# 528 small products and three 32x32 turns appended behind the last image

## The chip, the cores and the metric

The kernel runs on one core of one Trainium2 chip. The metric is the device time of one execution in microseconds (us). A profile of one execution is read beside it: its span runs from the first to the last instruction that the profiler recorded on the core.

## The reference

Thirty-two images of 384 channels and 28 x 28 points, in float32, pass through two layers. Cut to what matters:

```python
# layer 0, per image
y = depthwise_conv_7x7(x) + dw_b
y = layernorm_over_channels(y) * ln_g + ln_b
y = gelu(einsum('bhwc,cf->bhwf', y, w1) + b1)      # 384 -> 1536
nx = gx / (mean(gx) + eps), gx = sqrt(sum over points of y*y)
y = grn_g * (y * nx) + grn_b + y
x = x + einsum('bhwf,fc->bhwc', y, w2) + b2        # 1536 -> 384
# layer 1, per image
logits = [mean(x) @ W1.T, max(x) grouped, min(x) @ W3.T] @ Wfc.T
out = sigmoid(logits[:, :, None, None] + x)
```

## The kernel before

The kernel has two stages. In the first (`with ExitStack() as one`), which the trace shows up to about 500 us, the depthwise convolution of all images is done on TensorE with banded matrices, channel by channel, and the sums of weight blocks that the second stage multiplies by are formed and stored in DRAM. In the second stage each image goes through `up(b)` (384 to 1536 channels) and `down(b)` (1536 to 384). Both use fast matrix multiplication schemes: sums of blocks of the data are formed by VectorE and GpSimd, and TensorE multiplies each by a sum of weight blocks. `up` has 15 products per weight block group on 392 columns (line 979), `down` has 38 steps of 3 products on 196 columns (line 1139). All are float32. The names that matter here:

- `u2_tiles`: five buffers for the weights of `down`; the first has 128 partitions of 768 numbers and is named `u` in the profile (the fifth lies in `ws`).
- `d_room`: 128 x 8820 numbers that hold the block sums of `down`. GpSimd writes them in `sums` (line 1102).
- `room`: a work area that the sums of the last image use as well.
- `bank(name)`: the next of eight PSUM banks of 512 float32 columns, handed out in turn.
- `down` ends each image's products by adding them from PSUM into the image `xt` on VectorE, and reduces it to sums, maxima and minima (`stq`, `st`).
- `gate_store(b)` multiplies these by the gate weights on GpSimd (`zt`, line 1187), sums them over the partitions with one small product by ones (`pa`, line 1189), forms the logits on VectorE (`lt`, `lg`, lines 1193 and 1198), and applies the sigmoid on ScalarE, three times 128 x 784 (line 1200). For the last image each third is stored by SyncE as soon as it is ready (line 1204).

The order on each engine is mostly found by the framework's planner; an instruction wrapped in `tc.keep_in_program_order` keeps its place in the order in which the program was written. The last two lines of the loop over images, and the line behind it, are:

```python
        down(b, beside(b))
    gate_store(B - 1)
```

A float32 product of the program is one `nc.tensor.matmul`; the profile shows it as two records MATMUL, each with a LDWEIGHTS of its own in front.

Of the kernel before, what the change touches and what calls it, by code (L numbers as in the profile page):

```python
# [13 lines left out]
P = 128  # L14
# [4 lines left out]
HW = 28  # L19
# [12 lines left out]
PW = P // RW  # L32
# [183 lines left out]
def convnext_gate_kernel(  # L216
# [13 lines left out]
    nc = tc.nc  # L230
# [57 lines left out]
    room = const.tile([P, CB * NT + NA * NH], F32, name="room")  # L288
# [101 lines left out]
    with ExitStack() as one:  # L390
# [107 lines left out]
        keep = tc.keep_in_program_order  # L498
# [282 lines left out]
        for s in range(NK):  # L781
# [8 lines left out]
            if s in later:  # L790

                dst, src = later[s]
# [15 lines left out]
            if s == NK - 1:  # L808
# [19 lines left out]
                for half, (b0, b1) in enumerate(((0, B0), (B0, B))):  # L828
# [4 lines left out]
                    for n in range(2 * PAIRS):  # L833
                        i, c2 = divmod(n, PAIRS)
# [10 lines left out]
            elif s < NK - 2:  # L845
                for c2 in range(PAIRS):
# [9 lines left out]
                    elif q in (2 * PAIRS + 2, 2 * PAIRS + 5, 2 * PAIRS + 8):  # L856
                        n = FB + 4 * ((q - 2 * PAIRS) // 3)
# [35 lines left out]
    u2_tiles = [up2.tile([P, UD * KD * P], F32, name=f"u2_{i}") for i in range(NU2 - 1)]  # L893
# [6 lines left out]
    d_room = dp.tile([P, SLOTS * KD * NQ4], F32, name="d_room")  # L900
# [11 lines left out]
    def bank(name):  # L912
        nonlocal nbanks
        nbanks += 1
        return pszs[(nbanks - 1) // 4 % 2].tile([P, 512], F32, tag="pz", name=name)
# [265 lines left out]
    def gate_store(b):  # L1181

        xt, st = gates.pop(b)
        ov = out[b].rearrange("(cb p) n -> p cb n", p=P)
        n = NQ * R
        zt = smp.tile([P, NQ, R], F32, tag="zt", name=f"zt_{b}", bufs=1)
        nc.gpsimd.tensor_tensor(zt, gate, st.unsqueeze(2).to_broadcast([P, NQ, R]), ALU.mult)
        pa = bank(f"pa_{b}")
        nc.tensor.matmul(
            pa[:, :n], ones_f, zt.rearrange("p q r -> p (q r)"), start=True, stop=True  # L1190
        )
        lt = smp.tile([P, CB, n], F32, tag="lt", name=f"lt_{b}", bufs=1)
        nc.vector.tensor_tensor(
            lt, fct.rearrange("p cb q r -> p cb (q r)"),
            pa[:, :n].unsqueeze(1).to_broadcast([P, CB, n]), ALU.mult,
        )
        lg = smp.tile([P, CB], F32, tag="lg", name=f"lg_{b}")
        nc.vector.tensor_reduce(lg, lt, AX.X, ALU.add)
        for cb in range(CB):
            nc.scalar.activation(  # L1200
                xt[:, cb, :], xt[:, cb, :], AF.Sigmoid, bias=lg[:, cb : cb + 1], scale=1.0
            )
            if b == B - 1:
                nc.sync.dma_start(ov[:, cb, :], xt[:, cb, :])
        if b < B - 1:
            nc.scalar.dma_start(ov, xt)
# [3 lines left out]

    HF = FB // 2
    V, A = nc.vector, nc.scalar

# [11 lines left out]
    def squared(b):  # L1227

        return 0 if b == 1 else HF if b in (0, B - 1) else HF // 2

    def within(b):
        hooks, at = adder()
        p = b - 1
        if b == 0:
            at((0, 3), finish, 1)
            at((0, 13), finish, 2)
            at((0, 17), finish, 3)
            for i, m in enumerate(first_outs[:HF]):
                at((0, 29), stretch, m, nc.gpsimd)
# [8 lines left out]
        elif b == 1:  # L1248
            for i, m in enumerate(first_outs[HF:]):
                at((0, 2 * i), stretch, m, nc.gpsimd)  # L1250
# [10 lines left out]
        else:  # L1261
            for i, f in enumerate(order[HF:]):
                at((0, 5 + 2 * i), scale, p, f)
            for i in range(0, 13, 6):
                at((0, 4 + i), sums, p)
        if b > 1:
            for m in range(HF):
                at((2, 2 + 4 * m), gelu, b, m)
            for m in range(squared(b)):
                at((2, 29 if m >= HF // 2 else 22 + 2 * m), square, b, m)  # L1270
        if 2 <= b and b + 1 < B:
# [3 lines left out]
    def beside(b):  # L1275
        hooks, at = adder()
        n = b + 1
        last = n == B - 1

        def part(i):  # L1280

            return i * ND // 15

        if b + 2 < B:
            for cb in range(CB):
                at(2 + 3 * cb, normed, b + 2, (cb,))
            if b == 0:
                for i, d in enumerate(FORMS):
                    at(12 + 2 * i, forms_up, 2, (d[0],), V)
            else:  # L1290
                at("after sums", forms_up, b + 2)
        if n < B:
            g0 = 0 if n == 1 else HF
            for f in range(g0, FB):
                at(part((f - g0) // 3), gelu, n, f)
            s0 = squared(n)
            for f in range(s0, FB):
                at(part((1 if last else 3) + (f - s0) // 2), square, n, f)
        if n < B:
            at(part(4 if last else 9), grn, n)  # L1300
        if b >= 1 and not last:
            at(part(11) if n < B else ND - 8, gate_store, b - 1)
        if n < B:
            at(part(11) if b else 0, load_x, n)
        if last:
            for i, f in enumerate(order):
                at(part(4 + i // 3), scale, n, f, V if i % 3 == 2 else A)
            for i in range(part(7), ND):
                at(i, sums, n)
            if b >= 1:  # L1310
                at(part(9), gate_store, b - 1)
        elif n < B:
            for i, f in enumerate(order[:HF]):
                at(part(9) + 1 + i, scale, n, f)
        return hooks
# [14 lines left out]
    for b in range(B):  # L1330
        if b >= 1 and b + 1 < B:
            up(b + 1, within(b + 1))
        down(b, beside(b))
    gate_store(B - 1)


# [37 lines left out]
```

## Time and profile before

| | |
|---|---|
| median of the runs shown | 3040.19 us (two runs: 3039.02 and 3041.36) |
| the profiled execution, its own time | 3041.33 us |
| its span | 3039.6 us |
| granted TensorE clock, mean | 0.997 |
| TensorE products busy | 2996.2 us (99%), 14436 records |
| TensorE weight loads busy | 2427.9 us (80%), 14436 records |
| VectorE / ScalarE / GpSimd busy | 2036.2 / 1787.4 / 2431.9 us |
| last records: the product `pa` (line 1189) | starts at 3032.02 us |
| last sigmoid (line 1200) | ends at 3035.95 us |
| last data moved by the DMA engines | between 3038 and 3039 us |

Times inside the profile count from the start of the span. The granted clock is the share of full speed that TensorE's throttle passes, 1.00 being full. A record's duration covers the time from its start to the modelled end of its results; the next record can start earlier, so the distance from start to start, and not the duration, is what a stream of products costs.

### The profile page before, as it was taken

Reading aid. Unit: us, or ns where it says so; the run is one execution under the profiler, and the core shown is the slowest. Engines: PE = TensorE matmul, PEld = TensorE weight load, DVE = VectorE, ACT = ScalarE, POOL = GpSimd, SP = SyncE. Lnnn points to the kernel's source line nnn. Section 1 sums busy time; section 2 is a strip of 40 time slices with the busy share of each in tenths; the row PEclk is TensorE's granted clock in tenths of the full one; section 3 lists DMA queues with packets and bytes.
Section 4 is the critical chain, followed back from the end, with each engine's and each line's share of the span. In section 5 each row is a group of like instructions: output and inputs, shape, how many; then the busy total and the mean of one; then the engine's idle time right before and its main releaser. Section 6 shows DMA issues by size and latency. Waiting matters only on the chain.

```text
span 3039.6 us, 43826 instructions
## 1 busy us (share of the span) xinstructions
PE 2996.2 (99%) x14436; PEld 2427.9 (80%) x14436; DVE 2036.2 (67%) x4643; ACT 1787.4 (59%) x2899; POOL 2431.9 (80%) x1811
## 2 busy tenths in 40 slices
PE   8999999899999999999999999999999999999998
PEld 8999997577777777777777777777777777777777
DVE  5767667776666666666666666666666666666665
ACT  4455554756666666666666666665666666666661
POOL 3367866688888888888888888888888888888897
PEclk9999999999999999999999999999999999999999
DMA  9899997546666666666666565566655666666645
GB/s 358 327 359 375 364 342 259 169 149 203 199 206 207 201 204 207 199 206 207 199 206 207 198 205 194 199 203 204 195 191 196 197 198 200 201 203 201 195 152 198
DMA packets 279256, 674.94 MB, mean 222 GB/s; under 512 B 24234, under 2 KB 99704, under 8 KB 273016
## 3 DMA queue, kind: packets, MB, share of 16 engines
q1 hardware_dynamic: 266472, 634.63, 61.9%
q10 hardware_dynamic: 12560, 37.51, 3.1%
q8 instruction: 117, 1.92, 0.2%
q14 instruction: 107, 0.88, 0.1%
HBM read 575.57 MB, written 96.48 MB: 221 GB/s over the span
## 4 chain that ended last, share of the span: by engine, by line
PE 91%; POOL 3%; DVE 3%; DMA 2%; issue 1%; ACT 1%; SPq 0%; ACTq 0%; DVEq 0%; POOLq 0%
PE ph_C L979 13%; PE ph_A L979 12%; PE ph_B L979 12%; PE pz_A L1139 8%; PE pz_C L1139 8%; PE pz_D L1139 7%; PE pz_F L1139 7%; PE pc L718 5%; PE pc L720 4%; PE pc L722 4%; PE pt L516 2%; PE pz_H L1139 2%; PE pz_I L1139 2%; POOL d_room L1102 2%; PE pz_E L1139 2%; DVE room L344 1%
## 5 line engine op out<-in xcount | busy, mean ns | idle before, releaser
L355 ACT ACTIVATE y<-y,vecs,gsc 128x784 f32<-128x784 f32 x375 | 359.9, 1030 | 467.0 <-DVE gsc L1047 467.0
L1102 POOL TENSOR_TENSOR d_room<-y 128x588 f32<-128x588 f32 x250 | 360.1, 1444 | 294.4 <-PE pz_B L1139 217.7
L927 ACT ACTIVATE y<-y,b1f 128x784 f32<-128x784 f32 x384 | 350.4, 945 | 196.7 <-DVE y L998 174.7
L979 PE MATMUL ph_C<-room,ws 128*128 128x392 f32 x1224 | 456.6, 494 | 4.1 <-DVE y L996 2.9
L1102 POOL TENSOR_TENSOR d_room<-d_room,y 128x588 f32<-128x588 f32 x308 | 442.8, 1442 | 16.7
L979 PE MATMUL ph_B<-room,ws 128*128 128x392 f32 x1220 | 451.7, 492 | 2.3 <-DMA ws<-u1d 2.3
L979 PE MATMUL ph_A<-room,ws 128*128 128x392 f32 x1220 | 453.0, 492 | 0.1
L979 PEld LDWEIGHTS ph_C<-room,ws 128*128 128x128 f32 x1224 | 230.6, 190 | 182.2 <-DVE y L996 21.7
L979 PEld LDWEIGHTS ph_A<-room,ws 128*128 128x128 f32 x1220 | 231.6, 190 | 170.5 <-POOL room L386 0.8
L979 PEld LDWEIGHTS ph_B<-room,ws 128*128 128x128 f32 x1220 | 231.0, 190 | 164.0 <-DMA ws<-u1d 2.9
L741 POOL TENSOR_TENSOR stats<-stats,sq 128x896 f32<-128x896 f32 x96 | 200.8, 2092 | 176.6 <-ACT sq L735 175.9
L947 ACT ACTIVATE stats<-y 128x784 f32<-128x784 f32 x381 | 326.7, 858 | 9.1
L1102 POOL TENSOR_TENSOR d_room<-y,d_room 128x588 f32<-128x588 f32 x214 | 306.5, 1438 | 27.0 <-PE pz_D L1139 15.9
L386 POOL TENSOR_TENSOR room<-room 128x392 f32<-128x392 f32 x298 | 298.9, 1019 | 11.6
L735 ACT ACTIVATE sq<-yt,dwb 128x224 f32<-128x224 f32 x368 | 157.2, 474 | 223.3 <-DVE yt L725 212.9
L1102 POOL TENSOR_TENSOR y<-y 128x588 f32<-128x588 f32 x180 | 258.3, 1435 | 6.5
L994 DVE TENSOR_TENSOR y<-y,ph_B 128x392 f32<-128x392 f32 x252 | 135.6, 558 | 157.9 <-ACT y L927 123.5
L992 DVE TENSOR_TENSOR y<-y,ph_C 128x392 f32<-128x392 f32 x386 | 213.4, 561 | 25.0 <-PE ph_C L979 0.3
L725 DVE STREAM_TRANSPOSE yt<-pc 128x448 f32<-128x448 f32 x184 | 119.3, 648 | 138.0 <-PE pc L722 99.5
L1139 PE MATMUL pz_A<-d_room,u 128*128 128x196 f32 x1050 | 204.4, 330 | 0.4 <-DMA u<-u2d 0.2
L718 PE MATMUL pc<-xt,tmat 128*128 128x224 f32 x736 | 200.8, 355 | 0.6 <-ACT xt L527 0.6
L1139 PEld LDWEIGHTS pz_A<-d_room,u 128*128 128x128 f32 x1050 | 178.4, 190 | 8.6 <-POOL d_room L1102 0.9
(299 smaller groups left out, 6410.8 us busy)
## 6 DMA issues: line engine op xcount, KB each, us to landing
u<-u2d SPq DMA_DIRECT2D x487, 384.0 KB, 3.7
ws<-u1d SPq DMA_DIRECT2D x380, 320.0 KB, 3.0
tmat<-fs SPq DMA_DIRECT2D x47, 1420.0 KB, 10.5
ws<-u2d SPq DMA_DIRECT2D x121, 384.0 KB, 3.8
yi<-yd SPq DMA_DIRECT2D x95, 448.0 KB, 6.4
yd<-yt SPq DMA_DIRECT2D x47, 896.0 KB, 7.0
x<-in_x SPq DMA_DIRECT2D x32, 1176.0 KB, 5.4
out<-x ACTq DMA_DIRECT2D x31, 1176.0 KB, 6.3
```

The source lines that it names most:

```text
L355: eng.activation(out, in_, AF.Identity, bias=add, scale=mul)
L386: tc.keep_in_program_order(eng.tensor_tensor(d, o[in0], o[in1], op))
L718: keep(nc.tensor.matmul(po, t[:, c, P : 2 * P], xc, start=True, stop=False))
L735: nc.scalar.activation(sq[:, cy % SQ + ci], yt[:, cy + ci], AF.Square, bias=dwb[:, cc + ci : cc + ci + 1], scale=1.0,)
L741: ins = nc.gpsimd.tensor_tensor(ssum, ssum, sq, ALU.add)
L927: ins = nc.scalar.activation(y, y, AF.Gelu, bias=b1f[:, f : f + 1], scale=1.0)
L947: ins = nc.scalar.activation(stats[:, :NT], ys[b][:, f, :], AF.Square, accum_out=ssqs[b][:, f : f + 1])
L979: ins = nc.tensor.matmul(banks[t, bk][:, :NH], wts[t, g][:, gi, :], o[opnd], start=(first == 1), stop=True, skip_group_check=True,)
L992: ins = nc.vector.tensor_tensor(d, d, p, ALU.add)
L994: ins = nc.vector.tensor_tensor(d, d, p, ALU.subtract)
L1102: eng.tensor_tensor(d[0], o[a][0], o[c][0], ALU.add if sign == "+" else ALU.subtract)
L1139: nc.tensor.matmul(pz[:, :NQ4], wt[:, i % UD, t, :], o[opnd][0][:, t, :], start=(first and t == 0), stop=(t == KD - 1), skip_group_check=True,
```

## The change

One function is added and called once behind the last `gate_store`. It takes four PSUM banks (`tiled_0` to `tiled_3`) and issues 528 products in nine groups. Each multiplies a piece of `d_room` by a piece of the first weight buffer; both hold whatever the last image left there. A product's rows (the partitions that are summed over) start at partition `r`, and its columns are written to PSUM partitions from `j`. In the program each product carries the part of TensorE's 128 x 128 array that it uses: `tile_size` [rows, columns] and `tile_position` [r, j]. Nothing reads the four banks. Then VectorE turns 32 x 32 blocks of three overlapping pieces of `d_room` into `room`, which nothing reads afterwards either. The output is computed as before.

```diff
+    def tiled_products():
+
+        keep = tc.keep_in_program_order
+        probes = [bank(f"tiled_{i}") for i in range(4)]
+        nw = 0
+
+        def product(r, nr, j, ncol, out_bank, n, back=False):
+            nonlocal nw
+            w0 = 32 * (nw % 20)
+            m0 = 32 * (nw % 64)
+            nw += 1
+            rows_, cols_ = slice(r, r + nr), slice(j, j + ncol)
+            rhs = d_room[rows_, m0 : m0 + n]
+            if back:
+                rhs = rhs.rearrange("p (a b) -> p a b", b=28)[:, ::-1, ::-1]
+            keep(
+                nc.tensor.matmul(
+                    probes[out_bank][cols_, :n], u2_tiles[0][rows_, w0 : w0 + ncol], rhs,
+                    start=True, stop=True, skip_group_check=True,
+                )
+            )
+
+        for i in range(8):
+            for j in range(4):
+                product(0, P, 32 * j, 32, i % 4, 280)
+        for i in range(4):
+            for j in range(4):
+                for r in range(4):
+                    product(32 * r, 32, 32 * j, 32, r, 448)
+        for i in range(4):
+            for r in range(4):
+                for j in range(4):
+                    product(32 * r, 32, 32 * j, 32, r, 448)
+        for i in range(6):
+            for j in range(4):
+                for r in range(4):
+                    product(32 * r, 32, 32 * j, 32, r, 196)
+        for i in range(4):
+            for j in range(4):
+                for r in range(4):
+                    product(32 * r, 32, 32 * j, 32, r, 196, True)
+        for i in range(6):
+            for j in range(4):
+                for r in range(4):
+                    product(32 * r, 32, 32 * j, 32, r, 112)
+        for i in range(10):
+            for r in range(4):
+                product(32 * r, 32, 0, P, r, 224)
+        for i in range(6):
+            for j in range(4):
+                for r in range(2):
+                    product(64 * r, 64, 32 * j, 32, 2 * r + i % 2, 224)
+        for i in range(6):
+            for j in range(2):
+                for r in range(2):
+                    product(64 * r, 64, 64 * j, 64, 2 * r + i % 2, 224)
+        src = d_room[:, : HW * HW + 4]
+        for i in range(3):
+            src = d_room[:, i * 800 : i * 800 + HW * HW + 4]
+            view = bass.AP(
+                tensor=src.tensor, offset=src.offset, ap=[src.ap[0], [HW, HW], [1, PW]]
+            )
+            keep(
+                nc.vector.transpose(
+                    room[:, i * HW * PW : (i + 1) * HW * PW].rearrange("p (a b) -> p a b", b=PW), view
+                )
+            )
...
     gate_store(B - 1)
+    tiled_products()
```

## The prediction

> **What bounds the kernel now.** I read the page's busy shares first, then the chain of work that ended last, then its final twelve microseconds, because the whole change stands behind the last image.
>
> ```profile
> PE 2996.2 (99%) x14436; PEld 2427.9 (80%) x14436; DVE 2036.2 (67%) x4643; ACT 1787.4 (59%) x2899; POOL 2431.9 (80%) x1811
> PE 91%; POOL 3%; DVE 3%; DMA 2%; issue 1%; ACT 1%; SPq 0%; ACTq 0%; DVEq 0%; POOLq 0%
> ```
>
> TensorE is busy 99% of the span and carries 91% of the chain. So whatever TensorE gets behind its last record is added to the end, unless it fits beside what still follows there. What follows, in the chain of the last stretch (start, duration, what):
>
> ```profile
> 3031.30 0.23 DVE st L1176 x3
> ...
> 3032.02 0.46 PE pa L1189 x2
> 3032.48 0.02 issue
> 3032.50 0.39 DVE lt L1193
> 3032.89 0.02 issue
> 3032.91 0.39 DVE lg L1198
> 3033.30 0.02 issue
> 3033.33 0.95 ACT x L1200
> 3034.28 0.84 ACTq L1370
> 3035.11 0.84 ACT x L1200
> ```
>
> The reader is to see that TensorE's last product is `pa`, at 3032.02, and that logits, three sigmoids and three stores fill the remaining 7.6 us to the span's end at 3039.6. This is the only cover that the change has.
>
> For the price of a product I took the chain in a full stretch of `down` and of `up`:
>
> ```profile
> 3023.81 0.99 PE pz_H L1139 x6
> 3024.80 0.99 PE pz_D L1139 x6
> ```
>
> ```profile
> 2922.26 1.32 PE ph_A L979 x4
> 2923.58 1.32 PE ph_B L979 x4
> ```
>
> Six records of 196 columns start within 0.995 us (starts 3021.60 and 3020.60 tell the third digit), 165.8 ns each; four of 392 columns within 1.317 us, 329.2 ns each. The line through both is 0.834 ns a column plus 2.4 ns. Records of 192 and 224 columns in the first stage (162 and 189 ns) lie on it. A program's float32 product is two such records, one behind the other, each with its own weight load, which hides under the record before (loads of 128 columns last 190 ns, yet the starts stay 166 ns apart).
>
> **The change part by part.** It removes nothing and adds no DMA, and moves no instruction: in the changed kernel's order of instructions all 528 products stand on TensorE behind `pa`, and the three turns on VectorE behind `lg`. The first product waits for an earlier product of TensorE itself, long done, and nobody waits for the products or the turns.
>
> *The turns.* The trace has the turn of 128 x 448 numbers at 648 ns (line 725); one of 896 is then about 1.3 us, three 3.9 us. They start behind `lg`, at 3033.3, and end at 3037.2, beside the stores and the products: nothing on the path. Without that cover they would cost 3.9 us.
>
> *The instructions.* TensorE's 28872 records go with an instruction queue of 1.92 MB in 117 packets, about 67 bytes a record; 2112 more (two products and two loads each) are 9 packets. Spread over the products' time they come at least as seldom as one in some 13 us. I take zero; if each stopped TensorE for the 2.5 us that the nearest transfer takes to land (a store of 392 KB), 22 us.
>
> *The products, one after another.* Two records each by the line above:
>
> | group | products x columns | us |
> |---|---|---|
> | 128 x 32 parts | 32 x 280 | 15.1 |
> | 32 x 32, rows change first | 64 x 448 | 48.1 |
> | 32 x 32, columns change first | 64 x 448 | 48.1 |
> | 32 x 32 | 96 x 196 | 31.8 |
> | 32 x 32, read backwards | 64 x 196 | 21.2 |
> | 32 x 32 | 96 x 112 | 18.4 |
> | 32 x 128 | 40 x 224 | 15.1 |
> | 64 x 32 | 48 x 224 | 18.2 |
> | 64 x 64 | 24 x 224 | 9.1 |
> | sum | 528 | 225.1 |
>
> *How many run at once* is what this trace does not show: all its streams use the whole array (the nearest, three records of 24 rows, are single and use all 128 columns). From below: sixteen 32 x 32 parts fit the array, eight of 64 x 32, and four of each other size, so 167.6/16 + 18.2/8 + 39.3/4 = 22.6 us. From above: no overlap, 225.1 us; above that, if a load is not hidden and each record's results are waited for: 163 ns (329 less 166) and about 109 ns (the loads of 128 and 96 columns, 190 and 164 ns, continued to 32) on each of 1056 records, 287 us more.
>
> I take **two at once**, 112.6 us. The reason is the two records of a product. In the rows above records start in written order, and the second record of a product needs the part of the array that the first is still streaming through. So if starts stay in order, the second record waits for the first, and only the next product, in another part, can start beside it. Then each product costs one record instead of two. Every two neighbours of the nine groups use different parts, so this holds in all of them. To it I add one emptying of the pipe, 163 ns, at each of the five changes of the part's size: 0.8 us. Between two-fold and serial lies a weight load seen once per product, 109 ns x 528 = 58 us.
>
> [...]
>
> *The clock.* The trace shows its price:
>
> ```profile
> 2988.00:2990.00 2.00, 0.04 (x1) 0.07 (x1) 1.97 (x5) 0.00 (x0) 2.00 (x2) 0.93 0.97 386
> 2990.00:2992.00 2.00, 2.00 (x6) 2.00 (x7) 0.54 (x2) 0.00 (x0) 2.00 (x3) 0.50 0.20 80
> ```
>
> Here the seventh number of a stretch is the granted clock. After 5.0 us without a product (from 2984.96) it fell to 0.50, and six records of 196 columns took 2.09 us instead of 0.995, until it rose after some 3 us. In the last stretch it fell at about 3034.1; before, TensorE had only `pa` since 3029.8. The products fill the time from 3032.2, so I count full speed; a fall at the start would cost at most some 1.6 us.
>
> *Sum.* The first product starts at 3032.2 (`pa` holds TensorE for 0.17 us in the chain at 3022.59). 3032.2 + 112.6 + 0.8 + 0.2 for the last results is 3145.8, against 3039.6: plus 106.2 us. On the profiled execution's 3041.33 us that is 3147.5; this execution was 1.1 us above the median of 3040.19, so the median would be 3146.4. I say **3147 us**, 3.5% slower.
>
> **The rivals.**
>
> *No overlap.* Small parts are worth nothing here, or a stretch of float32 holds the whole array. For it: every record in this trace starts when the one before has streamed. Against it: the neighbours share no rows or no columns of the array. 3032.2 + 225.1 + 1.0 = 3258.3: plus 218.7, **3259 us**.
>
> *Four or more at once*, the rival on the other side. If each part has its own queue, the second record of a product does not hold the next one back. Four at once take 56.3 us: 3032.2 + 56.3 + 1.0 = 3089.5, plus 49.9, **3090 us**, 1.6%, not slower by 2%. It decides from 3.3 at once, where the products take 68 us. With all parts at once (22.6 us) it is 3056 to 3057 us. Against it are the two records of each product; nothing in the trace speaks for more than two.
>
> *Dearer than serial.* The throttle does not take a product in one sixteenth of the array for work: two-fold at half clock is 2.1 x 112.6 = 236 us, **3270 us**, serial at half clock 473 us, 3506 us; or the loads and results come into sight, up to 512 us, 3545 us. Against it: the clock stayed at 1.00 through stretches with a few narrow products (96 columns of weights, at 480 us), but no part was as small.
>
> *The change does nothing*, because what nobody reads is dropped: the order of instructions has all 528, so I give it no share.
>
> **How the numbers follow.** Two at once, with or without a load in sight (3147 to 3205): 0.50. No overlap: 0.20. Four at once: 0.15. More than four: 0.05. Dearer than serial: 0.10. The range takes in the first three, 3085 to 3265, which leaves 0.15 out. Two per cent, about what a measurement of this kernel can tell from no change, is 61 us: slower by more has the first, second and fifth case, 0.80; within it the others, 0.19; 0.01 is left for faster, since nothing is taken away.
>
> **What the changed profile would show.** Right: TensorE's `tiled` records start at 3032.2; two of them start per record time, so 96 products of 196 columns take about 16 us and 64 of 448 about 24; both groups of 448 take the same; the clock stays at 1.00; sigmoids, stores and turns keep their places and end by 3040. Wrong: the group where columns change first takes twice the one where rows change first (then only rows overlap), groups at the serial figure or at a quarter of it, or a granted clock of 0.50 behind 3034.

## The result

The changed kernel takes 3073.41 us, median of two runs (3072.26 and 3074.56), against 3040.19 us before: ratio 1.0109, 95% interval 1.0066 to 1.0153. A second comparison, told of below, gave 1.0098 (1.0081 to 1.0114). The kernel is slower by 30 to 33 us, half of the 2% that a reader would call a clear change and a third of the 106 us that were forecast. The time lies outside the forecast range, on its low side.

The busy line of the page and the line of TensorE's instruction queue (packets, MB, share) after the change:

```profile
PE 3029.8 (99%) x15492; PEld 2451.7 (80%) x15492; DVE 2039.9 (66%) x4646; ACT 1787.4 (58%) x2899; POOL 2433.4 (79%) x1811
...
q8 instruction: 125, 2.05, 0.3%
```

The records are 1056 more on TensorE, two for each of 528 products, and three on VectorE. The queue brought 8 packets more than the 117 before.

The chain that ended last, from `pa` on (start, duration, what):

```profile
3033.85 0.70 PE pa L1189 x2
3034.55 15.03 PE tiled L1229 x387
3049.58 0.49 issue
3050.07 2.34 PE tiled L1229 x108
3052.41 1.13 issue
3053.55 2.20 PE tiled L1229 x99
3055.75 1.55 issue
3057.30 1.78 PE tiled L1229 x95
3059.08 1.97 issue
3061.05 10.89 PE tiled L1229 x234
```

Logits, sigmoids and stores have left the chain; from `pa` to the end it is only products, and four stretches, 5.1 us in all, in which TensorE was idle and waited for nothing that the profile shows. `pa` itself starts at 3033.85 instead of 3032.02: 1.8 us of the difference of these two executions arose before the first added instruction. From the start of `pa` to the end of the span it is 39.0 us instead of 7.6. (The chain counts only the records that lie on it: x108 there is 128 records in the trace.)

The nine groups, one line for each in the order of the diff (start and end, length, TensorE busy, weight loads busy, granted clock, share of the DMA engines, GB/s):

```profile
3034.48:3039.76 5.28, 5.28 (x65) 2.28 (x65) 0.73 0.49 191
3039.76:3043.26 3.50, 3.50 (x133) 2.31 (x132) 1.00 0.16 61
3043.26:3047.04 3.78, 3.78 (x152) 2.83 (x130) 1.00 0.02 4
3047.04:3051.26 4.22, 3.73 (x214) 2.94 (x195) 1.00 0.03 8
3051.26:3054.73 3.47, 2.34 (x143) 1.68 (x139) 1.00 0.02 5
3054.73:3061.50 6.77, 3.26 (x207) 2.37 (x197) 0.98 0.01 2
3061.50:3067.00 5.50, 5.50 (x84) 5.07 (x80) 0.72 0.01 3
3067.00:3069.43 2.43, 2.43 (x100) 1.86 (x96) 1.00 0.03 7
3069.43:3071.93 2.50, 2.50 (x56) 1.73 (x48) 1.00 0.00 0
```

All products took 37.45 us. The two groups of 448 columns, 48.1 us each one after another, took 3.50 and 3.78: by an estimate from these figures some 13 products at once (48.1/3.50 = 13.7, 48.1/3.78 = 12.7). The three short groups (lines 4 to 6) took 14.46 us for 71.4 us of serial work, and TensorE was not even busy in all of it. The first and the seventh ran at a mean clock of 0.73 and 0.72.

The turns and the stores stand where they were expected, some 2 us later, as `pa` was (timeline, same execution: start, duration, engine, what):

```profile
3035.30 3.09 DVE L1276 STREAM_TRANSPOSE room<-d_room 128x896 f32<-128x896 f32 x3
...
3036.39 2.01 SPq L1204 DMA_DIRECT2D out<-x  x3
```

### The profile page after: what moved, and what is told of

Its sections match the earlier page's. It is cut to its first block, busy times and chain, and to the rows that moved or that the text cites. A ratio compares the mean times of both kernels' runs of the same rounds, so it can differ in the third digit from the quotient of the medians.

```text
span 3072.8 us, 45942 instructions
## 1 busy us (share of the span) xinstructions
PE 3029.8 (99%) x15492; PEld 2451.7 (80%) x15492; DVE 2039.9 (66%) x4646; ACT 1787.4 (58%) x2899; POOL 2433.4 (79%) x1811
## 4 chain that ended last, share of the span: by engine, by line
PE 92%; DVE 3%; DMA 3%; POOL 1%; issue 1%; ACT 0%; SPq 0%; DVEq 0%; POOLq 0%; ACTq 0%
PE ph_C L979 13%; PE ph_A L979 12%; PE ph_B L979 12%; PE pz_A L1139 8%; PE pz_C L1139 8%; PE pz_D L1139 7%; PE pz_F L1139 7%; PE pc L718 4%; PE pc L720 4%; PE pc L722 4%; PE pz_H L1139 2%; PE pz_I L1139 2%; PE pt L516 2%; PE pz_E L1139 2%; DVE room L344 1%; PE tiled L1229 1%
## 5 line engine op out<-in xcount | busy, mean ns | idle before, releaser
L1102 POOL TENSOR_TENSOR d_room<-d_room,y 128x588 f32<-128x588 f32 x308 | 443.1, 1443 | 16.7
```

The source lines that it names most:

```text
L1102: eng.tensor_tensor(d[0], o[a][0], o[c][0], ALU.add if sign == "+" else ALU.subtract)
```

## The experiments

Three questions were open: why so many products ran at once although each has two records in one part; what the gaps without a visible wait are; and with what use of the array the clock falls. Group times below are from the first record of a group to the first of the next.

### Where the overlap comes from: all products in one part

```diff
-            rows_, cols_ = slice(r, r + nr), slice(j, j + ncol)
+            rows_, cols_ = slice(0, nr), slice(0, ncol)
```

> All 528 products keep their sizes, but each takes the first rows and the first columns of the array, so that neighbours share one part. Theory A (products run at once because they lie in different parts): nothing overlaps any more, the products take the serial 225 us instead of 37.4 us, and the kernel some 3261 us. Rival (neighbours overlap wherever they lie, since they wait for nothing and write four banks): 37 us as now, 3073 us.

Measured: 3463.63 us. The stretches of the 528 products (columns as above): first group, first 3.7 us of the second, rest of the second, third, all others.

```profile
3033.49:3048.70 15.21, 15.21 (x64) 6.96 (x64) 1.00 0.21 80
3048.70:3052.40 3.70, 3.70 (x11) 1.08 (x11) 1.00 0.00 0
3052.40:3140.65 88.25, 88.25 (x120) 20.36 (x119) 0.50 0.00 0
3140.65:3236.22 95.57, 95.57 (x130) 22.08 (x128) 0.50 0.00 0
3236.22:3461.04 224.82, 224.82 (x737) 141.80 (x735) 0.50 0.00 0
```

The overlap is gone: the first group takes 15.21 us, and the serial price worked out for it was 15.1. At full clock the records of the second group start 376 ns apart, which is the price of one record of 448 columns by the prediction's line (0.834 x 448 + 2.4); so in this run the two records of a product ran one after the other. What neither expectation had is the clock, which fell to 0.50 at 3052.41 and never rose again: 427.5 us instead of 225. That is the prediction's rival of serial products at half clock (473 us), and this run, with all products in one part, came near it.

### Two, and all, of a part's products in a row

The loops were turned so that each part gets two products (`run = 2`), or all of its group's products (`run = 0`), before the next part:

```diff
+        def spread(n, parts):
+            for i0 in range(0, n, run or n):
+                for part in parts:
+                    for i in range(i0, min(n, i0 + (run or n))):
+                        yield i, part
...
-        for i in range(4):
-            for j in range(4):
-                for r in range(4):
+        for i, (r, j) in spread(4, rj):      # rj: the pairs (r, j), r changing first
                     product(32 * r, 32, 32 * j, 32, r, 448)
```

> The same products in the same parts, but each part gets two products directly one behind the other (four records). Theory A1 (every part has a queue of its own, and a record that waits for its part holds back no record of another part): 37 to 41 us of products, 3073 to 3078 us. Rival A2 (records start in the written order, and the one that waits holds the next; in the changed kernel something else brings the two records of a product apart): three record times for two products, 0.75 x 225 = 169 us, 3205 us. Between them if the engine looks only some records ahead.

Measured: 3077.93 us, 40.8 us of products; the two groups of 448 columns:

```profile
3038.44:3044.50 6.06, 6.06 (x131) 4.02 (x136) 1.00 0.35 136
3044.50:3050.69 6.19, 6.19 (x141) 4.22 (x131) 1.00 0.02 5
```

The total is that of theory A1, but the groups are neither as before (3.50) nor at the 36 us of A2: 48.1/6.06 is 7.9 products at once. In the trace the first eight records of the group start within 94 ns, the next eight from 401 ns on. With all products in one part the records started 376 ns apart, so I take those eight to lie in eight parts (the trace does not name a record's part); the eighth part's first record is the 29th in the written order, and it started 300 ns ahead of records written before it. The next part's first record starts at 586 ns, just after the first record of all has ended (its duration is 559), and the one after that at 962. From these starts I estimate that some 32 records of the written order were open to a start at a time: the 29th started with the first eight, the 33rd only at 586 ns.

> The same products in the same parts, but each part gets all of its group's products directly one behind the other (4 to 10). Theory A3 (the engine looks 16 products, 32 records, ahead, and whatever in that window has a free part starts): as many parts run at once as 16 products cover, 2 for eight in a row, 4 for four, 2.7 for six, 1.6 for ten; the groups of 448 columns take 12.0 us each (3.5 now, 6.1 with two in a row), all products 75 us, 3111 us. Rival A4 (each part can hold only the records of two products, and the third blocks what follows): two parts at once in the long runs, 24 us for a group of 448 columns, some 110 us of products, 3147 us. Rival A1 (no limit): 37 to 41 us, 3074 to 3078 us.

Measured: 3262.54 us. First group, the two of 448 columns, all others:

```profile
3034.79:3047.26 12.47, 12.47 (x65) 5.91 (x65) 1.00 0.25 98
3047.26:3072.54 25.28, 25.28 (x130) 8.36 (x130) 1.00 0.00 1
3072.54:3117.31 44.77, 44.77 (x131) 11.17 (x129) 0.53 0.00 0
3117.31:3259.94 142.63, 142.63 (x739) 95.36 (x735) 0.54 0.00 1
```

The second group, at full clock, took 25.28 us, near the 24 of rival A4: records start at 0, 400, 776, 1151, then at 1527 and 1533, 1903 and 1933. Only with the fifth record, at 1527 ns, does another start beside it, at 1533. My estimate from these starts is that here no more than four records of one part were open at a time, the running one among them, and that a fifth held what followed. Then each part runs all but its last four records before the next part comes in. For the second group (sixteen parts with eight records of 0.376 us) that makes 16 x 4 x 0.376 + 4 x 0.376 = 25.6 us, and for the first (four parts with sixteen records of 0.236 us) 4 x 12 x 0.236 + 4 x 0.236 = 12.3 us, against 25.28 and 12.47 measured. The 12.0 us that A3 gives from 32 records alone do not fit the 25.28 us here; in the run before, no part had more than four. No run shows the 32 or the four directly: both are estimates that fit these starts and group times. Beyond the second group the clock was at 0.50 for 174 us, which neither had.

Whether the engine itself takes records out of the written order, or whether the program's last translation places them so, was not tried.

### What the gaps are

In the changed kernel the gaps stand exactly 128 records and their 128 loads apart, 256 instructions (timeline: start, length, what, records, idle time before):

```profile
3050.07 2.34 PE L1229 MATMUL tiled<-d_room,u 32*32 32x196 f32 x128 [0.49 <-issue]
3053.55 2.20 PE L1229 MATMUL tiled<-d_room,u 32*32 32x196 f32 x128 [1.13 <-issue]
3057.30 1.78 PE L1229 MATMUL tiled<-d_room,u 32*32 32x112 f32 x128 [1.55 <-issue]
```

The view of the DMA engines from 3047 to 3061.5 us (40 slices) shows what moved then:

```profile
GB/s 0 45 0 0 0 0 0 0 0 0 0 45 0 0 0 0 0 0 0 0 0 45 0 0 0 0 0 0 0 0 0 0 45 0 0 0 0 0 0 0
...
q8 instruction: 4, 0.07, 1.7%
```

Four packets of instructions, 10 to 11 slices or 3.6 to 4.0 us apart, and nothing else. Each packet is moved within 0.9 to 1.2 us. TensorE resumes 1.4 to 1.5 us after one has landed, and the next begins to move 1.1 to 1.3 us after that: a round of 3.5 to 4.0 us for 256 instructions, 64 float32 products. In the groups of 448 columns, where no gap stands, most starts are 16 to 17 ns apart, 16.7 on the average.

```diff
-        for i in range(6):
+        for i in range(12):
             for j in range(4):
                 for r in range(4):
                     product(32 * r, 32, 32 * j, 32, r, 112)
```

> The group of 96 products of 112 columns is issued twice (192). Theory B (TensorE's instructions come in packets of 256, one packet per 3.5 to 3.75 us, and a float32 product has four): 96 more products are 384 instructions, plus 5.3 to 5.6 us over the changed kernel, 3079 us. Rival B1 (the array's time sets it, sixteen at once): plus 96 x 0.191 / 16 = 1.2 us, 3074.6 us. Rival B2 (a start every 16.7 ns, as in the groups of 448 columns): plus 3.2 us, 3076.6 us.

Measured: 3076.34 us (3075.03 to 3077.77), ratio to before 1.0112 (1.0095 to 1.0129). The group of 112 columns took 10.86 us for 192 products instead of 6.77 for 96. As time, the 4.1 us more of this group lie between theory B and rival B2 and settle nothing; as a rate, 10.86 us is three packets of 3.62 us, with five gaps (6.3 us) instead of four.

```diff
-                    product(32 * r, 32, 32 * j, 32, r, 196)
+                    product(32 * r, 32, 32 * j, 32, r, 448)
...
-                    product(32 * r, 32, 32 * j, 32, r, 112)
+                    product(32 * r, 32, 32 * j, 32, r, 448)
```

> The 256 products of 196 and 112 columns get 448 columns each; their number stays. Theory B (supply of instructions): these groups take 14.4 us in the changed kernel and 14.0 to 15 us now, with 2.8 times the columns; 3071 to 3074 us, the lower end if the clock no longer falls behind them. Rival B1 (the array's time, sixteen at once): 4.5 us become 12.0, plus 7.5 us, 3081 us.

Measured: 3070.77 us (3068.16 to 3075.09), ratio 1.0096 (1.0081 to 1.0112). The 256 products with 448 columns each took 15.17 us (14.46 with 196 and 112), and the clock did not fall. Two to four times the columns cost 0.7 us in the groups and nothing in the total.

The sharpest of these runs keeps the instructions and doubles the products. The 96 float32 products of 112 columns became 192 in bfloat16, of other data:

```diff
+        d_half, u_half = ones_f.bitcast(half), ident.bitcast(half)
+        for i in range(12):
...
-                    product(32 * r, 32, 32 * j, 32, r, 112)
+                    nc.tensor.matmul(probes[r][32 * j : 32 * j + 32, :112],
+                        u_half[rows_, 32 * (n % 8) : 32 * (n % 8) + 32],
+                        d_half[rows_, 32 * (n % 4) : 32 * (n % 4) + 112], ...)
```

> In place of the 96 float32 products of 112 columns stand 192 in bfloat16 (of the constants of ones and of the identity matrix, 32 x 32 parts, rows change first). If a bfloat16 product is one record with one load, these are the same 384 instructions for twice as many products. Theory B (supply): the group takes 5.5 to 6.8 us, as the 96 did. [...] Rival B2 (a start every 16.7 ns): 3.2 us, the gaps smaller by as much.

Measured: 3070.52 us. A bfloat16 product is one record with one load (192 of each in the trace). From the first to the record behind the group 6.6 us passed; the chain there:

```profile
3051.18 0.53 PE tiled L1261 x35
3051.71 1.69 issue
3053.41 1.25 PE tiled L1261 x128
3054.65 2.50 issue
```

128 records, with their loads 256 instructions, are through in 1.25 us, and then TensorE is idle for 2.50. The 128 records started on the average 9.8 ns apart, so B2's 16.7 ns is no floor for them. The same 384 instructions took 6.6 us as 192 products and 6.77 as 96: theory B.

The groups of 196 and 112 columns left out:

> The three groups of 196 and 112 columns are left out (256 products, 14.5 us in the changed kernel). Theory B (supply of instructions): the gaps in which TensorE waits for nothing in the trace are gone, and with them the fall of the clock behind them, so the 32 x 128 group takes 4.0 us instead of 5.5; some 20 us of products, 3055 us. Rival (the gaps come after some 15 us of small products whatever they are): two or three gaps remain, 3 to 5 us more, 3058 to 3060 us.

Measured: 3053.7 us, 20.6 us of products, no gap, and the 32 x 128 group at 4.00 us with the clock at 1.00. As theory B had it (20 us, 3055 us).

Only the group of 112 columns, and the turns:

> Of the products only the 96 of 112 columns are left, directly behind the last image, and the three turns. Theory B (supply, with some 350 to 500 instructions in store when they begin): they take 3.2 us (a start per 16.7 ns) to 4.5 us instead of the 6.8 us that they take behind the other groups, end before the last store lands, and the kernel's time is that of the kernel before, 3041 us, plus 0. Rival B1 (array's time): 1.2 us, the same total. Rival B3 (this form is slow by itself): 6.8 us, which ends at about the same time as the stores, plus 0 to 1 us.

Measured: 3041.36 us, ratio to before 0.9998 (0.9989 to 1.0008). 96 products behind the last image cost nothing. In the profiled execution they took 5.15 us: the clock was at 0.50 for the first half of it, and one gap of 1.33 us came before the last ten records. They ended 5.8 us after `pa` began, while the stores were still to land. The total cannot tell the theories apart, as each had said.

The short groups ahead of the others, in the order 112, 196, 196 backwards:

> The same nine groups, the one of 112 columns first, then the two of 196, then the others in their order. Theory B (supply): the short groups begin with 350 to 500 instructions in store and take 9 to 11 us instead of 14.5, and the slower groups behind them need fewer instructions than arrive; all products 32 to 34 us instead of 37.4, 3068 to 3070 us. Rival (each group has its own time wherever it stands): 37.4 us, 3073 us.

Measured: 3066.61 us, 34.9 us of products. The short groups still took 14.08 us (timeline as above):

```profile
3029.13 2.50 PE L1229 MATMUL tiled<-d_room,u 32*32 32x112 f32 x182
3033.00 2.31 PE L1229 MATMUL tiled<-d_room,u 32*32 32x112 f32 x128 [1.37 <-issue]
3037.85 5.43 PE L1229 MATMUL tiled<-d_room,u 32*32 32x196 f32 x202 [2.54 <-issue]
```

The first gap came after 182 records with their loads, some 365 instructions, as it did in the run before (182 of 192 records). These 365 lie within the 350 to 500 of theory B, but the gain did not come: 14.08 us instead of 9 to 11. TensorE resumed at 3033.00, and the next packet began to move only at 3035.56, 2.56 us later instead of 1.1 to 1.3; why is open. Behind the second gap the clock was at 0.50 for 3.4 us. The rest of the difference to the changed kernel is the first and the 32 x 128 group at full clock, 3.91 and 4.00 instead of 5.27 and 5.50, less 0.7 us that the groups of 448 columns took longer.

The first row bears on rival B2 as well. With its instructions at hand TensorE started those 182 records within 2.24 us, 12 ns each, so 16.7 ns is no floor for float32 records of 112 columns either.

### The turns alone

The nine groups left out, the turns kept:

> All products are left out; the three turns stay behind the last image. They take 3.1 us on VectorE behind the logits and end before the last store lands: 0, within what a comparison can tell. Rival (the turns or the wider program delay the stores or the end): plus 3 us.

Measured: 3040.4 us, ratio 0.9996 (0.9987 to 1.0006); they run from 3032.53 to 3035.62 in the profile, beside the sigmoids.

### The clock and the part of the array in use

In the changed kernel's trace the stretches at 0.50 lasted 3.41 us (from 3033.88 and from 3061.19) and, in front of the products, 6.82 us (from 2989.51). In place of the groups, nine stretches, each behind 16 products in the whole array and each with one kind of use:

```diff
+        for name, nr, ncol, n, times in (
+            ("col_strip", P, 32, 280, 32), ("row_strip", 32, P, 224, 40),
+            ("quarter", 64, 64, 224, 40), ("eighth", 64, 32, 224, 40), ("single", 32, 32, 448, 20),
+        ):
+            whole()
+            to = bank(name)
+            for _ in range(times):
+                product(to, 0, nr, 0, ncol, n)
+        for name, nr, ncol, in (("two_rows", 2, 1), ("two_cols", 1, 2), ("four_rows", 4, 1), ("four_cols", 1, 4)):
...
+                        product(to[r], 32 * r, 32, 32 * j, 32, 448)
```

> In place of the nine groups, nine stretches of some 15 us each at full clock, each behind 5.3 us of products in the whole array: one part at a time (128 x 32, 32 x 128, 64 x 64, 64 x 32, 32 x 32), then two and four 32 x 32 parts at once, once in different rows and once in different columns. The turns are left out. Theory C (the throttle counts how much of the array is at work): 32 x 32 alone falls to 0.50 some 3.4 to 6.8 us into its stretch and takes up to 27 us; a quarter of the array (128 x 32, 32 x 128, 64 x 64, four parts) keeps 1.00; 64 x 32 and two parts are open. Rival C1 (it counts the time in which any record runs): no stretch falls, and the fall in the run with all products in one part has another cause. Rival C2 (it counts rows at work): 128 x 32 and four in different rows keep 1.00, 32 x 128 and four in different columns fall. By theory C some 200 us of products in all, 3235 to 3250 us.

Measured: 3280.95 us. The nine stretches in that order (length, TensorE busy, granted clock, DMA share, GB/s):

```profile
3037.94:3053.15 15.21, 15.21 (x65) 1.00 0.03 10
3058.66:3084.95 26.29, 26.29 (x81) 0.58 0.00 1
3092.91:3108.18 15.27, 15.27 (x81) 1.00 0.00 1
3113.69:3128.93 15.24, 15.24 (x81) 1.00 0.01 1
3134.44:3161.20 26.76, 26.76 (x41) 0.56 0.00 0
3168.59:3183.74 15.15, 15.15 (x81) 1.00 0.01 1
3189.25:3216.22 26.97, 26.97 (x82) 0.56 0.00 1
3223.41:3238.57 15.16, 15.16 (x161) 1.00 0.00 1
3244.08:3271.29 27.21, 27.21 (x161) 0.55 0.00 1
```

As rival C2 had it. Each of the five stretches with 64 or 128 rows at work stayed at 1.00 (128 x 32, 64 x 64, 64 x 32, two and four parts in different rows). Each of the four with 32 rows fell (means 0.55 to 0.58), though 32 x 128 and four parts in a row strip fill a quarter of the array, twice what 64 x 32 fills. Theory C does not fit, and C1 neither, since TensorE was busy throughout. Four stretches fell where theory C had one, at 11 to 12 us each, which is why the total lies above its 3235 to 3250 us. The 32 rows alone were always rows 0 to 31. The run with all of a group in a row agrees: its second group, in which neighbouring parts have different rows, kept 1.00 for 25.28 us; in the third, where they share their rows, the clock fell after 2.6 us.

### The changed kernel again

> The changed kernel once more, beside the kernel before on the same chip. The sum of its groups stays (7.3 us for the two groups of 448 columns, 14.5 for the three short ones); what may differ is whether the clock is at 0.50 during the first group and the 32 x 128 group, 1.4 and 1.5 us. Ratio 1.009 to 1.012; if the gaps had been an accident of one execution, the short groups would take 5 us less.

Measured: 3071.81 us (3070.17 to 3074.65), ratio 1.0098 (1.0081 to 1.0114). No fall of the clock in this execution: first group 3.91 us, 32 x 128 group 4.00. Groups of 448 columns 3.50 and 3.79, short groups 15.47 us with gaps of 1.05, 1.41, 1.82 and 1.96 us. All products 35.6 us.

## Why the prediction was wrong

**What bounds the kernel and what covers: right.** The products begin right behind `pa` and the whole cover is what followed it, 7.6 us. The turns cost nothing.

**The serial sum: right.** 15.21 us against 15.1 for the first group in one part, and half clock made the rest about twice its price.

**How many run at once: wrong, and the step that failed.** The step said that the second record of a product, waiting for its part, holds back the next product, so that two run at once. It did wait (376 ns from start to start with all products in one part), but it did not hold the next product back: some 13 products ran at once in the changed kernel, 7.9 with two of a part's products in a row, 1.9 with four (48.1/25.28). The nine groups of the change come round to the same part after 4 to 16 products with two records each, so neither the 32 records nor the four to a part that I estimated from the starts should bind hard. Without the three short groups the products took 20.6 us, where all parts at once need 96.2/16 + 18.2/8 + 39.3/4 = 18.1 us, and two at once 77. The rival with all parts at once, which had the lowest share of the three kinds of overlap, had this term nearly right: 22.6 us. Starts in the written order, from which the two-fold followed, do not fit the first eight records within 94 ns with two products in a row, unless the order was changed before TensorE got them. For the changes of the part's size the sum had 0.8 us: in the changed kernel's trace the first record behind each of the five starts 0.28 to 0.35 us after the last one before it, 1.5 us in all and some 70 ns before that record's modelled end, while groups of one size follow each other within 17 ns.

**The instructions: mis-sized.** I took zero, with 22 us as the other end, on the ground that packets would come no more often than one in 13 us. That followed from the 112 us of the wrong step. In the changed kernel the 128 records between two gaps took 1.78 to 2.34 us, less than the 3.5 to 4.0 us from packet to packet. The three short groups took 14.46 us where the array needs 71.4/16 = 4.5: 10.0 us. Not all of this need be the supply. Between the gaps the records of 196 and 112 columns start some 15.5 and 12 ns apart on average, by which their 512 records would take an estimated 7.3 us with all instructions at hand; so the supply cost, by this estimate, between 7.2 and 10.0 us.

**The clock: mis-sized.** At the start I counted full speed and 1.6 us at most; the first group lost 1.4 us (5.27 against 3.91). A second fall, behind the gaps of the short groups, cost the 32 x 128 group 1.5 us (5.50 against 4.00); the prediction did not have it. Another execution had neither. One reading was off: the pause behind which the clock fell in the kernel before lasted 4.6 us from the start of the last record (2985.37) to the next (2989.96), 4.3 of them idle, not 5.0.

**The turns: off the path, as forecast, and mis-sized.** Each took 1.03 us instead of 1.3, 3.09 in all instead of 3.9.

The account of the 37.45 us: 22.6 for the array with all parts at once (the prediction's estimate), 10.0 for the short groups beyond it, most of it the supply of instructions, 2.9 for the clock, and 1.9 for the rest, of which 1.3 lie in the groups of 448 columns (7.28 against 6.0). Whether these 1.3 come from the starts within the groups or from the supply, whose rate is nearly the same there (64 products in 3.50 us), was not separated. 37.45 us and some 1.5 us around them, less the cover of 7.6, are the 31.4 us by which the stretch from `pa` to the end grew.

## What to carry to other kernels

Let neighbours in the written order use different parts: here float32 products in 32 x 32 parts then ran some 13 at once where a part came back only after the others, 8 with two of its products in a row, 2 with four. Then price the instructions before the columns: here 256 arrived per 3.5 to 4.0 us, so that a float32 product in a 32 x 32 part cost 55 to 60 ns with 112, 196 or 448 columns, and the long ones were the cheaper ones by the column. Look at the rows at work: here 64 and more kept the clock at 1.00 for 15 us, and 32 took 26 to 27 us for work of 15, the clock falling to 0.50 (nothing between 32 and 64 rows was run).

## What was not expected of the hardware

- The granted clock went with the rows at work. 64 x 32 for 15.24 us kept 1.00; 32 x 128 and four 32 x 32 parts in one row strip fell to 0.50 within about 4 us (an estimate from 26.29 and 27.21 us for work of 15.2). It was not seen to rise with 64 rows: with all products in one part the 64 x 32 and 64 x 64 groups (36.0 and 18.2 us) stayed at 0.50.
- TensorE stood idle for 0.1 to 2.5 us at a time, in the changed kernel 128 records and 128 loads apart, while only packets of instructions moved (four in 14.5 us); the chain of waits shows this as time in which the engine waits for nothing. In the kernel before, with 117 packets, such time is 1% of the chain.
- 128 bfloat16 records of 32 x 32 parts and 112 columns were through in 1.25 us, 9.8 ns each.
